# Three PSUM banks for scores, four for everything else, and one tile for a step's weights in a Perceiver cross-attention

## The chip, the core and the metric

The kernel runs on one core of one Trainium2 chip. The metric is the device time of one execution in microseconds (us), the median of several runs. A profile is one further execution, recorded instruction by instruction. Engines are named as the profile names them: PE (TensorE matmuls), PEld (TensorE weight loads), DVE (VectorE), ACT (ScalarE), POOL (GpSimd) and SP (SyncE, which issues most transfers).

## The reference, cut to what matters

The program is two layers of a Perceiver-like model over `x` of shape (4, 256, 256) with a context of shape (4, 4096, 192). Each layer is cross-attention to the context, a self-attention-like block, and a feed-forward block. The change touches only the first block, layer 0's cross-attention:

```python
x = x + _L0_xattn_ref(_layernorm(x), ctx_768, mask, Wq, Wk, Wv, Wo)
# 16 heads of 16 channels; for each of the 4 batches and each head:
#   scores  = (xn @ Wq) @ (ctx @ Wk).T / 4        256 tokens x 4096 context rows
#   weights = softmax(scores, masked rows left out)
#   out     = (weights @ (ctx @ Wv)) @ Wo
```

Everything is in float32.

## The kernel before, in words

**Units and steps.** `l0_xattn` cuts the work into 16 units: 4 batches times 4 groups of 4 heads. A unit's softmax needs the largest score of every token before it can exponentiate, so each unit's scores are computed twice. The first time (`ps_a`, tokens on the partitions, 512 context rows at a time) only the maximum of each row is kept (`mx`, L473). The second time (`ps_s`, context rows on the partitions, 256 tokens at a time) the negated maximum is already one of the rows of the query (`qb`), and ScalarE takes the exponential of what arrives (`e`, L469). These exponentials are the weights; they are multiplied with the values (`o_ps`, L406). One column of ones in the values gives the softmax's denominator.

**Half-steps.** One call of `step` is one sixteenth of a unit's exponentials and one sixteenth of another unit's maxima. The maxima run `LEAD` = 18 steps ahead of the exponentials, so the two belong to different units. `step` runs two halves, `hp` = 0 and `hp` = 1. A half has, on TensorE and in this order: the first score matmul of two heads (`weigh(0)`), one maxima matmul of each of the two other heads, the second score matmul of the first two heads (`weigh(1)`), and then `sums(hp)`, the four matmuls that multiply weights of the *previous* step with values. The four heads of a unit lie on the four groups of 32 rows of the systolic array, so the scores of two heads and the maxima of two others can stream through the array side by side. After the matmuls of a half ScalarE takes two exponentials and VectorE two maxima.

**PSUM.** Of the eight banks, one (`acc`) gathers `o_ps`, and seven form a ring (`ring`, tag `mm`) that all others share: two `ps_s` and two `ps_a` in each half, and between the steps the pair `ps_k0`/`ps_k1` or `ps_v0`/`ps_v1` of a projection of the context (28 key parts and 56 value parts within the steps), the transposed maxima `ps_m`, the queries `ps_q`, the tokens `ps_t`, the denominators `den` and the output projection `ps_wo`. A tile's first matmul has to wait until the last reader of the tile that held its bank is done.

**Weights.** Each head of a step has a tile of its own, `e0` to `e3`, with two buffers each. `ew` is the list of the four.

**Who sets the order.** The kernel is written with a tile framework. It decides the order of each engine's instructions from the program's order and its own estimate of when buffers come free, gives each tile a buffer, and adds the semaphore waits. An instruction that has to wait for two engines is preceded by a separate wait instruction (EVENT_SEMAPHORE in the trace). [...]

**The start.** In the first 18 steps (`t` < 0) there are no exponentials: each step has four `ps_a` matmuls alone, and from the tenth of them on one part of the first values (`first_values`) follows each.

Of the kernel before, what the change touches and what calls it, by code (L numbers as in the profile page):

```python
# [11 lines left out]
F32 = mybir.dt.float32  # L12
# [4 lines left out]
AF = mybir.ActivationFunctionType  # L17
ALU = mybir.AluOpType
AX = mybir.AxisListType
PSUM = bass.MemoryType.PSUM  # L20

P = 128
B, S, D = 4, 256, 256
# [224 lines left out]
def l0_xattn(c, w):  # L248
# [8 lines left out]
    nc, tc = c.nc, c.tc  # L257
    W = 17
    LEAD = 18
    with ExitStack() as es:  # L260
        one = es.enter_context(tc.tile_pool(name="x0_one", bufs=1))
        ring = es.enter_context(tc.tile_pool(name="x0_ring", bufs=7, space=PSUM))
        acc = es.enter_context(tc.tile_pool(name="x0_acc", bufs=1, space=PSUM))
        two = es.enter_context(tc.tile_pool(name="x0_two", bufs=2))

        def bank(name):
            return ring.tile([P, 512], F32, tag="mm", name=name)
# [128 lines left out]
        def sums(k):  # L396

            if not late:
                return
            u, n, ew = late.pop(0)  # L400
            b, g = divmod(u, 4)
            if n == 0:
                o_pss[u] = acc.tile([P, 512], F32, tag="o", name="o_ps")
            for h in range(4):
                c0 = (n * 8 + 4 * (g % 2) + h) * W
                nc.tensor.matmul(  # L406
                    o_pss[u][32 * h : 32 * h + 32, :S],
                    vs[g // 2][:, c0 : c0 + 32],
                    ew[h][:, n % 2, :],
                    start=(n == 0),  # L410
                    stop=(n == GT - 1),
                )
            if n == GT - 1:
                finish(u)
# [3 lines left out]
        def finish(u):  # L418
            b, g = divmod(u, 4)
            on = one.tile([P, S], F32, tag=f"on{g}", name=f"on{g}")  # L420
            attn_finish(c, two, ring, o_pss.pop(u)[:, :S], on)
            ons.append(on)
            if g == 3:
                add_projected(c, ring, b, ons, w.wo)
                ons.clear()

        def step(s, a):

            ew = {}
            for hp in range(2):  # L430
                work = []
                ts, ta = {}, {}
                for j in range(2):
                    if s:
                        ts[2 * hp + j] = bank("ps_s")
                    if a:
                        ta[2 - 2 * hp + j] = bank("ps_a")

                def weigh(k):
                    u, kp = s  # L440
                    for h, ps in ts.items():
                        hs = slice(32 * h, 32 * h + 32)
                        ks = slice((2 * kp + k) * P, (2 * kp + k + 1) * P)
                        nc.tensor.matmul(  # L444
                            ps[:, k * S : (k + 1) * S],
                            kts[u % 4 // 2][hs, u % 2, ks],
                            qbs[u][hs, :],
                            start=True,
                            stop=True,
                        )  # L450

                if s:
                    weigh(0)
                if a:
                    u, tt, ch = a
                    for h, ps in ta.items():
                        hs = slice(32 * h, 32 * h + 32)
                        nc.tensor.matmul(  # L458
                            ps,
                            qas[u][hs, tt * P : (tt + 1) * P],  # L460
                            kts[u % 4 // 2][hs, u % 2, ch * 512 : (ch + 1) * 512],
                            start=True,
                            stop=True,
                        )
                if s:
                    weigh(1)
                    for h, ps in ts.items():
                        e = two.tile([P, 2, S], F32, tag=f"e{h}", name=f"e{h}")
                        nc.scalar.activation(e, ps.rearrange("p (k n) -> p k n", k=2), AF.Exp)  # L469
                        ew[h] = e  # L470
                if a:
                    for h, ps in ta.items():
                        nc.vector.tensor_reduce(mxs[u][:, tt, h, ch : ch + 1], ps, AX.X, ALU.max)  # L473
                sums(hp)
            if s:
                late.extend((s[0], 2 * s[1] + k, ew) for k in range(2))

        n = 16 * 16
# [5 lines left out]
        for t in range(-LEAD, n):  # L484
            if t < 0:
                i = t + LEAD
                if i in (0, 2):
                    next(first_keys, None)
                if i == 3:
                    w.others()  # L490
                    for j in range(2):
                        nc.gpsimd.memset(kts[1][:, j, :], 1.0)
                if i > 8:
                    next(first_values, None)
            u, kp = divmod(t, 16)
            ua, ka = divmod(t + LEAD, 16)
            if ua < 16 and ka == 0 and ua > 0:
                queries(ua)
            if ua < 15 and ka == 8 and ua % 4 == 3:
                tokens(ua // 4 + 1)  # L500
            step((u, kp) if t >= 0 else None, (ua, ka % 2, ka // 2) if ua < 16 else None)
            if ua < 16 and ka == 15:
                with_largest(ua)
            if u in projections:
                steps, nb, ngp = projections[u]
                if kp == 0 and u % 2 == 0:
                    mask(nb, ngp)
                if kp % 2 == 0 if u % 2 else kp % 4 == 0:
                    next(steps, None)
        for _ in range(2):  # L510
            sums(0)
# [1376 lines left out]
def program(tc, a, out):  # L1888
# [3 lines left out]
    with ExitStack() as es:  # L1892
# [17 lines left out]
        with tc.tile_pool(name="w_a0", bufs=1) as pool_a0:  # L1910
            with tc.tile_pool(name="w_x0", bufs=1, side="right") as pool:
                w = l0_xattn_weights(c, pool)
                l0_xattn(c, w)
                w_a0 = l0_attn_weights(c, pool_a0)
            pool_f0 = es.enter_context(ExitStack())
            w_f0 = l0_ffn_weights(c, pool_f0.enter_context(tc.tile_pool(name="w_f0", bufs=1, side="right")))
            with tc.tile_pool(name="s4", bufs=1, side="right") as pool:
                l0_attn(c, w_a0, partial(s4d_kernel, c, pool))
# [148 lines left out]
```

## Time and profile before

| | |
|---|---|
| time, three runs | 2672.54 us median (2669.84 to 2682.69) |
| profiled execution: its own time | 2677.02 us |
| profiled execution: span from first to last instruction | 2674.9 us |
| the first 18 steps, maxima alone (about) | 25 to 102 us of the span |
| steps with scores and maxima | 102 to 1212 us |
| last steps, scores alone | 1212 to 1274 us |
| granted TensorE clock, 102 to 1274 us | 1.00 |
| 102 to 1274 us: busy PE, DVE, ACT | 1145.1, 663.0, 625.2 of 1171.9 us |
| exponentials (L469) | 1024, 594 ns each |
| maxima (L473) | 1024, 686 ns each |

The span is counted from the first instruction to the last; the time of a run has about 2 us more. A matmul in float32 is recorded as two passes, so counts of matmuls in the profile are twice those of the program. A row of the timeline merges neighbouring instructions of one kind: it gives the start of the first, the time from the first start to the last end, and the count. In brackets stands the idle time of that engine before the row and which engine's event ended it. The ends of matmuls are modelled.

### The profile page before, as it was taken

How to read it: one execution, taken by the hardware profiler on the slowest of the kernel's cores; microseconds unless marked ns; L12 is line 12 of the kernel's file. 1: busy time of each engine (PE TensorE's matmuls, PEld its weight loads, DVE VectorE, ACT ScalarE, POOL GpSimd, SP SyncE). 2: the span in 40 equal slices, each digit the busy share in tenths (PEclk: the TensorE clock that was granted, in tenths of full speed). 3: DMA queues.
4: the chain of work that ended last, by engine and by line, in shares of the span. 5: the costliest groups of instructions: out<-in, count | busy, mean ns of one | idle time of the engine just before them, and what ended most of it. 6: DMA issues, size and time to landing. Idle time of an engine off the chain costs nothing. (4 is left out here: it accounts for less than half of the span.)

```text
span 2674.9 us, 47755 instructions
## 1 busy us (share of the span) xinstructions
PE 2420.3 (90%) x19345; PEld 1419.5 (53%) x19345; DVE 1618.9 (61%) x3881; ACT 1095.0 (41%) x1913; POOL 179.1 (7%) x202
## 2 busy tenths in 40 slices
PE   8999999999999999999768989888999898984896
PEld 4445454545545454544435544466776777453554
DVE  6655655565565655561784440898798892735554
ACT  1355555555455555556111211555555562010221
POOL 3000000000000000000030000001010011412000
PEclk7899999999999999999888999799999999996876
DMA  7221213121221212100100012210303012100110
GB/s 197 76 53 58 61 50 80 38 73 45 62 56 55 63 37 73 45 2 1 43 1 1 5 47 67 79 60 20 99 22 97 6 50 96 55 0 16 33 24 8
DMA packets 63186, 130.78 MB, mean 49 GB/s; under 512 B 11584, under 2 KB 38912, under 8 KB 62512
## 3 DMA queue, kind: packets, MB, share of 16 engines
q1 hardware_dynamic: 61344, 123.73, 16.4%
q8 instruction: 154, 2.52, 0.4%
q10 hardware_dynamic: 1104, 2.88, 0.4%
q0 software_dynamic: 512, 1.05, 0.2%
q14 instruction: 72, 0.59, 0.1%
HBM read 97.12 MB, written 5.34 MB: 38 GB/s over the span
## 5 line engine op out<-in xcount | busy, mean ns | idle before, releaser
L473 DVE TENSOR_REDUCE mx<-ps_a 128x1 f32<-128x512 f32 x1024 | 658.3, 686 | 436.1 <-PE ps_a L458 436.1
L469 ACT ACTIVATE e<-ps_s 128x512 f32<-128x512 f32 x1024 | 555.8, 594 | 382.5 <-PE ps_a L458 356.5
L458 PE MATMUL ps_a<-kt,qa 32*128 32x512 f32 x2048 | 636.2, 653 | 1.9 <-DMA kt<-ks 0.8
L444 PE MATMUL ps_s<-qb,kt 32*128 32x256 f32 x4096 | 585.9, 401 | 0.0
L444 PEld LDWEIGHTS ps_s<-qb,kt 32*128 32x128 f32 x4096 | 348.7, 184 | 212.4 <-issue 94.2
L406 PE MATMUL o_ps<-e,v 128*32 128x256 f32 x4096 | 327.6, 391 | 0.0
L1152 PEld LDWEIGHTS ps_w<-diag,e 128*128 128x128 f32 x2048 | 238.8, 197 | 23.5 <-issue 21.5
L1152 PE MATMUL ps_w<-diag,e 128*128 128x128 f32 x2048 | 244.5, 281 | 0.4 <-POOL diag L1139 0.4
L458 PEld LDWEIGHTS ps_a<-kt,qa 32*128 32x128 f32 x2048 | 220.6, 186 | 20.9 <-DVE mx L473 7.8
L1109 DVE MAX8 cand<-sc 128x8 f32<-128x128 f32 x1024 | 212.2, 275 | 8.7 <-ACT sc L1097 8.7
L406 PEld LDWEIGHTS o_ps<-e,v 128*32 128x32 f32 x4096 | 81.0, 108 | 239.5 <-issue 229.5
L1133 DVE SCALAR_TENSOR_TENSOR e<-sc,top,e 128x1024 f32<-128x1024 f32 x128 | 159.1, 1279 | 28.5 <-ACT e L1124 28.5
L1124 ACT ACTIVATE e<-sc,neg 128x1024 f32<-128x1024 f32 x128 | 143.1, 1147 | 33.3 <-PE ps_w L1152 29.1
L1097 ACT COPY sc<-ps_s 128x1024 f32<-128x1024 f32 x128 | 126.3, 1007 | 41.9 <-PE ps_s L1088 39.6
L1166 PEld LDWEIGHTS ps_c<-cx,wT 128*128 128x128 f32 x512 | 86.1, 196 | 27.2 <-ACT wT L1160 11.3
L1166 PE MATMUL ps_c<-cx,wT 128*128 128x193 f32 x512 | 97.1, 341 | 1.9 <-ACT wT L1160 1.9
L335 ACT COPY v<-ps_v 128x256 f32<-128x256 f32 x128 | 41.4, 375 | 137.0 <-PE ps_v L325 137.0
L322 PE MATMUL ps_v<-x_wv,ctxT 128*128 128x128 f32 x512 | 92.8, 305 | 0.0
L322 PEld LDWEIGHTS ps_v<-x_wv,ctxT 128*128 128x128 f32 x512 | 69.4, 195 | 35.3 <-DVE mx L473 21.8
L1088 PE MATMUL ps_s<-kt,q 32*128 32x512 f32 x512 | 85.4, 647 | 0.0
L889 POOL MEMSET s_low<- 128x128 f32 x2 | 0.3, 206 | 1241.1 <-DVE x L188 1241.1
L301 ACT COPY ks<-ps_k 128x512 f32<-128x512 f32 x64 | 34.4, 589 | 111.4 <-PE ps_k L298 97.7
(403 smaller groups left out, 2735.6 us busy)
## 6 DMA issues: line engine op xcount, KB each, us to landing
ctxT<-in_ctxT SPq DMA_DIRECT2D x78, 768.0 KB
kt<-ks SPq DMA_DIRECT2D x352, 64.0 KB
cx<-in_ctx SPq DMA_DIRECT2D x16, 768.0 KB
x_w<-in_x_w SPq DMA_DIRECT2D x2, 1024.0 KB
qk<-rot SPq DMA_DIRECT2D x8, 256.0 KB
a_qk<-qk SPq DMA_DIRECT2D x16, 128.0 KB
ctxT<-in_ctxT ACTq DMA_DIRECT2D x2, 768.0 KB
x<-in_x SPq DMA_DIRECT2D x4, 256.0 KB
```

What stands on the lines that cost most here:

```text
L322: nc.tensor.matmul(ps[:, ks], ctxT[:, k0 : k0 + P], w.wv[:, 0, gs], start=True, stop=False)
L406: nc.tensor.matmul(o_pss[u][32 * h : 32 * h + 32, :S], vs[g // 2][:, c0 : c0 + 32], ew[h][:, n % 2, :], start=(n == 0), stop=(n == GT - 1),)
L444: nc.tensor.matmul(ps[:, k * S : (k + 1) * S], kts[u % 4 // 2][hs, u % 2, ks], qbs[u][hs, :], start=True, stop=True,)
L458: nc.tensor.matmul(ps, qas[u][hs, tt * P : (tt + 1) * P], kts[u % 4 // 2][hs, u % 2, ch * 512 : (ch + 1) * 512], start=True, stop=True,)
L469: nc.scalar.activation(e, ps.rearrange("p (k n) -> p k n", k=2), AF.Exp)
L473: nc.vector.tensor_reduce(mxs[u][:, tt, h, ch : ch + 1], ps, AX.X, ALU.max)
L1097: nc.scalar.copy(t, ps)
L1109: nc.vector.max(cands[u][:, n, :], sc[u][c4][:, i // 4, (i % 4) * P : (i % 4 + 1) * P])
L1124: nc.scalar.activation(t, src, AF.Exp, bias=neg)
L1133: nc.vector.scalar_tensor_tensor(t, src, top[:, 31:32], t, ALU.is_ge, ALU.mult)
L1152: nc.tensor.matmul(ps[:, i * P : (i + 1) * P], e[c4][:, half, i * P : (i + 1) * P], diag, start=(h == 0), stop=(h == 3),)
L1166: nc.tensor.matmul(ps_c[:, : DC + 1], wT[:, i * P : (i + 1) * P], cxs[b][t][:, j, :], start=(n == 0), stop=(n == 31))
```

## The change

It has two parts, both in `l0_xattn`.

1. The ring of seven banks becomes two pools. `three` has three banks and holds only the score tiles `ps_s`. `ring` keeps four banks and holds everything else: maxima, projections, transposed maxima, queries, tokens and denominators.
2. The four weight tiles `e0` to `e3` become one tile `e` of four heads per step, again with two buffers, so the memory is the same. The exponentials write, and the sums read, slices of it.

An unused list is removed too. The rest of the program is unchanged. Line numbers move by one at most: L406, L444 and L458 become L407, L445 and L459, the exponential stays L469, and the maximum L473 becomes L472.

```diff
-        ring = es.enter_context(tc.tile_pool(name="x0_ring", bufs=7, space=PSUM))
+        ring = es.enter_context(tc.tile_pool(name="x0_ring", bufs=4, space=PSUM))
+        three = es.enter_context(tc.tile_pool(name="x0_s", bufs=3, space=PSUM))
...
-                    ew[h][:, n % 2, :],
+                    ew[:, h, n % 2, :],
...
-            ew = {}
+            if s:
+                ew = two.tile([P, 4, 2, S], F32, tag="e", name="e")
             for hp in range(2):
-                work = []
                 ts, ta = {}, {}
                 for j in range(2):
                     if s:
-                        ts[2 * hp + j] = bank("ps_s")
+                        ts[2 * hp + j] = three.tile([P, 512], F32, tag="s", name="ps_s")
                     if a:
                         ta[2 - 2 * hp + j] = bank("ps_a")
...
                     for h, ps in ts.items():
-                        e = two.tile([P, 2, S], F32, tag=f"e{h}", name=f"e{h}")
-                        nc.scalar.activation(e, ps.rearrange("p (k n) -> p k n", k=2), AF.Exp)
-                        ew[h] = e
+                        nc.scalar.activation(ew[:, h, :, :], ps.rearrange("p (k n) -> p k n", k=2), AF.Exp)
```

## The prediction, made before the changed kernel had run

> **What bounds the kernel now.** I read the page first (who is busy), then the busy time by stretch, then the timeline of one plain stretch, then the built programs' waits.
>
> ```profile
> PE 2420.3 (90%) x19345; PEld 1419.5 (53%) x19345; DVE 1618.9 (61%) x3881; ACT 1095.0 (41%) x1913; POOL 179.1 (7%) x202
> L473 DVE TENSOR_REDUCE mx<-ps_a 128x1 f32<-128x512 f32 x1024 | 658.3, 686 | 436.1 <-PE ps_a L458 436.1
> L469 ACT ACTIVATE e<-ps_s 128x512 f32<-128x512 f32 x1024 | 555.8, 594 | 382.5 <-PE ps_a L458 356.5
> ...
> 102.15:1212.00 1109.85, 1084.87 (x10766) 558.48 (x10764) 659.48 (x1025) 585.36 (x1132) 0.00 (x0) 1.00 0.20 54
> ```
>
> VectorE and ScalarE both idle until TensorE delivers. In the 1110 us of steps with scores and maxima PE is busy 1085 at full granted clock, so TensorE sets the pace; but overlapped matmuls look busy while a later one waits, so I went to the timeline. These rows are two halves of a plain step:
>
> ```profile
> 599.93 0.48 PE L444 MATMUL ps_s<-qb,kt 32*128 32x256 f32 x2
> 599.94 0.70 PE L458 MATMUL ps_a<-kt,qa 32*128 32x512 f32 x2
> 600.47 0.59 PE L458 MATMUL ps_a<-kt,qa 32*128 32x512 f32 x2
> 600.68 0.38 PE L444 MATMUL ps_s<-qb,kt 32*128 32x256 f32 x2
> 601.10 1.29 DVE L473 TENSOR_REDUCE mx<-ps_a 128x1 f32<-128x512 f32 x2 [0.61 <-PE ps_a L458]
> 601.24 1.09 ACT L469 ACTIVATE e<-ps_s 128x512 f32<-128x512 f32 x2 [0.59 <-PE ps_a L458]
> 601.57 0.48 PE L444 MATMUL ps_s<-qb,kt 32*128 32x256 f32 x2
> 601.58 0.95 PE L458 MATMUL ps_a<-kt,qa 32*128 32x512 f32 x2
> 602.32 0.38 PE L444 MATMUL ps_s<-qb,kt 32*128 32x256 f32 x2
> 602.38 0.59 PE L458 MATMUL ps_a<-kt,qa 32*128 32x512 f32 x1
> 603.11 1.09 ACT L469 ACTIVATE e<-ps_s 128x512 f32<-128x512 f32 x2 [0.78 <-PE ps_a L458]
> 603.47 0.48 PE L444 MATMUL ps_s<-qb,kt 32*128 32x256 f32 x2
> ```
>
> Half A (hp 0) goes from 599.93 to 601.57: 1.64 us, nothing waits. Half B (hp 1) takes to 603.47: 1.90. Its two first `ps_a` passes are spread over 0.95 instead of 0.70 us: the second maxima matmul waits 0.26. The built program says for what: its bank is released by the *previous* half's first maximum (601.10 + 0.69 = 601.79, and the matmul starts 0.05 later). B's maximum starts later in the half, so the next A does not wait. A plain step is 1.64 + 1.90 = 3.54 us, of which 0.26 is this wait.
>
> **What the change does to the waits.** In the built changed program each bank's release can be followed. The maxima now reuse banks of two halves before, so the 0.26 us wait is gone. But each half takes two of three score banks, so in *every* half the second score matmul reuses the bank of the previous half's *first* score, and waits for its exponential. That is later than the first maximum: B's matmuls start at 601.57, the previous exponential has only begun at 601.24.
>
> What is queued behind: the second score matmul is second of a half's ten; both maxima, both `weigh(1)` and the sums follow it. TensorE lets nothing past:
>
> ```profile
> 846.01 0.29 PEld L458 LDWEIGHTS ps_a<-kt,qa 32*128 32x128 f32 x3 [0.35 <-DVE qa L377]
> 846.12 0.19 PEld L444 LDWEIGHTS ps_s<-qb,kt 32*128 32x128 f32 x2
> ```
>
> Here `ps_a` waited until 846.01 for new queries, and the weights of the next score matmul, on other rows of the array, came only after it (846.12 is 0.76 after the half's start, where 0.32 is normal). So the delay d of the second score matmul moves the whole half: its length is 1.63 + d.
>
> The value of d. The exponential starts 601.24, 1.31 after half A's start; one lasts 0.60 (merged two: 1.09); the release reaches TensorE 0.05 later, which these rows show (0.38 + 0.05 between copy and matmul):
>
> ```profile
> 859.35 0.38 ACT L169 COPY o_sb<-o_ps 128x256 f32<-128x256 f32 x1
> 859.78 0.70 PE L171 MATMUL den<-o_sb,sel 128*128 128x256 f32 x2 [0.97 <-ACT o_sb L169]
> ```
>
> 601.24 + 0.60 + 0.05 = 601.89, against 601.57: d = 0.32 in half B, had A been followed as in the changed kernel. If A was delayed itself, its exponential (which waits for the last maximum too, see the rivals) and its end move alike, so d stays. For half A the weights' tile matters. Before, nearly every exponential has a separate wait instruction (1016 of 1024), since it also waits for the earlier writer of its `e` buffer; after, in the built program, only the first of each step has (254). Half B's exponentials lose it. With it, ACT starts 0.14 to 0.18 us after the last maximum matmul's end (602.97 to 603.11; 601.06 to 601.24). Without it the nearest row is the copy of the values, 0.03 after its matmul (61.80 to 61.83, below). I take 0.07, since A's three near-simultaneous completions cost 0.03 more than B's: d = 0.32 - 0.10 = 0.22 in half A. Bounds: 0.15 (no latency at all) to 0.25.
>
> **The sum.** Laid out half by half over the timeline, this stretch has 237 halves A and 237 B. 135 A follow a B directly, 102 follow projections and the like (the exponential is then long done, d = 0); 102 B stand before such work.
>
> - 135 A and the 135 B before plain halves: now 478.2 us together (135 x 3.54). After: A 1.63 + 0.22 = 1.85, B 1.63 + 0.32 = 1.95, so 135 x 3.81 = 514. **+36**
> - 102 B before other work: 1.95 for 1.90. **+6**
> - Last 18 steps, scores alone, 1.63 a half, no waits now. Without maxima an exponential does not move with d, so what one half waits the next is spared: about 0.3 per step. **+5**
> - The start. With projections of values between maxima, now:
>
> ```profile
> 61.31 0.49 PE L325 MATMUL ps_v<-x_wv,ctxT 64*128 64x128 f32 x4
> 61.73 1.14 PE L458 MATMUL ps_a<-kt,qa 32*128 32x512 f32 x8
> 61.83 0.65 ACT L335 COPY v<-ps_v 128x256 f32<-128x256 f32 x2 [4.13 <-PE ps_v L325]
> 62.80 0.71 PE L322 MATMUL ps_v<-x_wv,ctxT 128*128 128x128 f32 x4
> 62.89 2.48 DVE L473 TENSOR_REDUCE mx<-ps_a 128x1 f32<-128x512 f32 x4 [1.35 <-PE ps_a L458]
> ```
>
> One step is 3.20 us (1.07 maxima, 2.13 values). Four `ps_a` and two `ps_v` fitted into seven banks; into four they do not. The values' second bank now waits for the step's second maximum. From its release: 1.80 of values left, 1.13 maxima, 0.04 wake, 0.61 + 0.68 for two maxima, 0.05: 4.31 instead of 3.20. Seven such steps: +8. Before them VectorE is the bound (0.6 us a maximum) and TensorE runs seven banks ahead; now four, so values start three maxima later: +2. **+10**
>
> Costed at nothing: the shared `e` tile. A buffer is reused every second step, and its last readers are the sums of the step just before, which TensorE has issued ahead of this step's first matmul; ScalarE starts 1.3 us after that. The sums read it by head (only the fourth waits, for an exponential done 0.5 us before). Were this a whole-tile wait, it would be the same exponential. Fourteen times the next half's scores move ahead of `den`; `den` waits about 1 us for ScalarE and the maxima still set the half's length: 0; if not covered, 0.5 x 14 = 7. SP's and POOL's order is unchanged, ScalarE has room (1.09 us of a half's 1.64).
>
> 36 + 6 + 5 + 10 = 57. The profiled execution would go from 2677.0 (span 2674.9) to 2734; its 4.5 us over the median of the runs stays, so **2672.5 + 57 = 2730**.
>
> **A rule weighed.** In the rows above the weights behind a waiting matmul wait with it. The Trainium skill ("TensorE: Matmul & The Clock Gate", Step-by-step: what each phase is for) says that TensorE pulls weight loads ahead of matmuls in flight when the row groups do not conflict. If that held during the wait, each delayed half would get back one load, 0.10 (the first two `ps_s` passes are 0.32 apart, later ones 0.22): 372 x 0.10 = 37, so +20 instead of +57. The trace's 846.12 speaks against it for an instruction waiting on a semaphore, so I keep 57 and leave 2693 in the range.
>
> **Rivals.**
> 1. *The change does what it seems to: the wait goes and none comes (not slower).* Mechanism: the exponential is released by its own score matmul, and the bank when its data are read (0.49, the spacing of two), not at its end (0.60). Own matmul ends 1.13 after the half's start whatever d is; 1.13 + 0.12 + 0.49 + 0.05 - 1.63 = 0.16 for a step's two d together. It decides where the two sum to under 0.27, the wait removed. Then 135 x -0.10 and 102 x -0.11, with +13 for start and end: -11, 2661; with the end at 0.60 about 2686. Against: in half B own scores end at 602.70, the maxima at 602.97, and ACT starts 603.11. It followed the maxima, which come earlier in TensorE's count.
> 2. *Weight loads run ahead:* 2693, above.
> 3. *Worse:* d 0.35 and 0.25 (more simultaneous completions), +53; end and start +7 and +15, the `den` reordering +5: +80, 2752.
> 4. *The change does not do what it says:* the built program shows three and four banks, and the wait instructions gone; excluded.
>
> **How the numbers follow.** About 0.5%, 13 us, is what a measurement of this kernel tells from no change. Forecast and its spread (2708 to 2752) 0.83; rival 2 and mixtures above 2686, 0.09; rival 1 0.08, of it 0.02 faster by over 13 us, 0.06 within. The bounds of d alone (0.15/0.26 to 0.25/0.35) make +27 to +75. Range 2697 to 2752.
>
> **What would show it.** Right: in plain stretches halves of about 1.85 and 1.95 us; the second `ps_s` weight load 0.2 to 0.3 after the first in every half; both `ps_a` of a half starting together; exponentials of half B starting under 0.1 after the last maximum; 102 becoming about 112, and the block's end 1274 about 1331; all later stages as long as before. Wrong: A and B at 1.64, or exponentials starting before the maxima end.

## Result: 3.3% slower, and the profile after

The changed kernel takes 2763.66 us (median of 6 runs, 2754.7 to 2772.19); the kernel before, on the same chip, 2671.95 us. The ratio is 1.0333, with a 95% interval of 1.0315 to 1.0352. The prediction was 2730 (2697 to 2752): the direction and the new wait were right, the size was not, and the time lies above the range. The profiled execution took 2763.01 us, its span is 2760.9 us against 2674.9. Some executions take a slower course at a lower mean clock (none of the kernel before's or the changed kernel's, but 1 of 6 of "busier start" and of "score matmul moved" below, 5 of 20 of "moved, values in score banks" and 4 of 14 of the last kernel), and every ratio leaves them out.

The page's busy rows after, and the groups that answer to those shown of before:

```profile
PE 2521.0 (91%) x19345; PEld 1536.0 (56%) x19345; DVE 1619.9 (59%) x3881; ACT 1094.6 (40%) x1913; POOL 184.6 (7%) x202
L472 DVE TENSOR_REDUCE mx<-ps_a 128x1 f32<-128x512 f32 x1024 | 659.4, 685 | 528.1 <-PE ps_a L459 527.8
L469 ACT ACTIVATE e<-ps_s 128x512 f32<-128x512 f32 x1024 | 555.7, 594 | 446.8 <-PE ps_a L459 417.2
```

No instruction of VectorE or ScalarE became longer: a maximum still takes 685 ns, an exponential 594. VectorE's idle time ahead of the maxima grew by 92 us (436.1 to 528.1), ScalarE's by 64: both wait longer for TensorE. TensorE's busy time grew by 101 us with the same 19345 records; since overlapping matmuls are merged, most of that is waiting that looks like work, and in the start, below, the passes themselves are longer.

The timeline of a plain stretch shows the wait:

```profile
619.90 1.09 ACT L469 ACTIVATE e<-ps_s 128x512 f32<-128x512 f32 x2 [0.87 <-PE ps_a L459]
620.23 0.81 PE L445 MATMUL ps_s<-qb,kt 32*128 32x256 f32 x3
620.56 0.19 PEld L459 LDWEIGHTS ps_a<-kt,qa 32*128 32x128 f32 x2
620.56 0.70 PE L459 MATMUL ps_a<-kt,qa 32*128 32x512 f32 x2
...
621.09 0.59 PE L459 MATMUL ps_a<-kt,qa 32*128 32x512 f32 x2
...
621.80 1.08 ACT L469 ACTIVATE e<-ps_s 128x512 f32<-128x512 f32 x2 [0.81 <-PE ps_a L459]
...
622.19 0.74 PE L445 MATMUL ps_s<-qb,kt 32*128 32x256 f32 x2
622.46 0.70 PE L459 MATMUL ps_a<-kt,qa 32*128 32x512 f32 x2
...
624.09 0.48 PE L445 MATMUL ps_s<-qb,kt 32*128 32x256 f32 x1
```

A half starts at 620.23 and its maxima only at 620.56; before, both started together. In between stands the second score matmul, which waits for the first exponential of the half before: 619.90 + 0.60 + 0.05 = 620.55. In the next half it is 0.27 (622.19 to 622.46; 621.80 + 0.60 + 0.05 = 622.45). The halves last 1.96 and 1.90 us, where they lasted 1.90 (B) and 1.64 (A). Both maxima now start together, so the wait of before is gone, as predicted.

The start went worse than predicted. This is one step with projections of values, and the first maxima of the next:

```profile
69.13 2.87 PE L459 MATMUL ps_a<-kt,qa 32*128 32x512 f32 x8
71.23 2.48 DVE L472 TENSOR_REDUCE mx<-ps_a 128x1 f32<-128x512 f32 x4 [4.30 <-PE ps_a L459]
71.98 1.10 PEld L323 LDWEIGHTS ps_v<-x_wv,ctxT 128*128 128x128 f32 x4 [1.56 <-DVE mx L472]
73.30 0.80 PE L326 MATMUL ps_v<-x_wv,ctxT 64*128 64x128 f32 x4
75.92 2.87 PE L459 MATMUL ps_a<-kt,qa 32*128 32x512 f32 x8
```

The weights of the first value bank wait 1.56 us for the first maximum, and those of the second bank wait again: instruction by instruction they start at 72.58, 0.05 after the second maximum ends (72.52). That is the predicted wait. But the step takes 6.79 us, not 4.31, and each pass is longer than before: four `ps_v` passes of L326 take 0.80 us, where they took 0.49. The busy time by stretch says why. Its columns are busy time with counts of PE, PEld, DVE, ACT and POOL, then the granted clock, the DMA share and GB/s; first two stretches of before, then two of after:

```profile
43.00:57.00 14.00, 14.00 (x50) 9.37 (x46) 12.21 (x27) 0.00 (x0) 0.00 (x0) 0.50 0.84 213
65.00:78.00 13.00, 13.00 (x100) 8.04 (x104) 10.15 (x17) 2.77 (x9) 0.00 (x0) 1.00 0.35 126
```

```profile
62.00:103.00 41.00, 41.00 (x148) 25.37 (x146) 14.89 (x24) 3.88 (x12) 0.00 (x0) 0.50 0.18 58
114.00:128.00 14.00, 12.98 (x44) 7.07 (x44) 8.02 (x13) 2.17 (x4) 0.00 (x0) 0.50 0.12 47
```

In both kernels the clock is at half in the last stretch of maxima ahead of the values. Before, it reached full some 7 us after the values had begun (53.19); after, it stayed at half until 128. In 62 to 103 PE looks busy all the time: this column tells neither a half clock nor a half empty array from work. Part of the array does wait: in the step above the third and fourth maxima matmul start 0.53 and 0.80 us after the first (69.65 and 69.93), each 0.05 after ScalarE's copy out of a value bank has ended.

Cut at the first plain half and at the last half of the last steps, the 86.0 us of the spans lie here (start, block, rest):

| part | before | after | difference | predicted |
|---|---|---|---|---|
| start, to the first plain half | 102.2 | 129.9 | +27.7 | +10 |
| plain halves A (136) | 1.64 | 1.90 (100), 2.09 (36) | +40.8 | +28 |
| plain halves B (135) | 1.89 | 1.96 | +9.4 | +8 |
| halves B before other work | | | +11 | +6 |
| other halves of the block | | | about 0 | 0 |
| last steps, scores alone | | | +3.3 | +5 |
| all later stages | 1402.8 | 1396.8 | -6.0 | 0 |

The code of the later stages is untouched; in the twelve profiles of this study they last from 1389 to 1406 us, so their 6 us mean nothing.

### The profile page after: what moved, and what is told of

It reads as the page before. It is cut to its first block, busy times and chain, and to the rows that moved or that the text cites. A ratio compares the mean times of both kernels' runs of the same rounds, so it can differ in the third digit from the quotient of the medians.

```text
span 2760.9 us, 46976 instructions
## 1 busy us (share of the span) xinstructions
PE 2521.0 (91%) x19345; PEld 1536.0 (56%) x19345; DVE 1619.9 (59%) x3881; ACT 1094.6 (40%) x1913; POOL 184.6 (7%) x202
## 5 line engine op out<-in xcount | busy, mean ns | idle before, releaser
L472 DVE TENSOR_REDUCE mx<-ps_a 128x1 f32<-128x512 f32 x1024 | 659.4, 685 | 528.1 <-PE ps_a L459 527.8
L469 ACT ACTIVATE e<-ps_s 128x512 f32<-128x512 f32 x1024 | 555.7, 594 | 446.8 <-PE ps_a L459 417.2
L445 PE MATMUL ps_s<-qb,kt 32*128 32x256 f32 x4096 | 707.3, 403 | 0.5 <-ACT e L469 0.5
L459 PE MATMUL ps_a<-kt,qa 32*128 32x512 f32 x2048 | 600.3, 669 | 1.7 <-DVE mx L472 1.6
L445 PEld LDWEIGHTS ps_s<-qb,kt 32*128 32x128 f32 x4096 | 465.7, 184 | 225.7 <-PE ps_a L459 91.8
L407 PE MATMUL o_ps<-e,v 128*32 128x256 f32 x4096 | 327.3, 391 | 0.0
L459 PEld LDWEIGHTS ps_a<-kt,qa 32*128 32x128 f32 x2048 | 176.4, 190 | 31.1 <-DVE mx L472 16.0
L407 PEld LDWEIGHTS o_ps<-e,v 128*32 128x32 f32 x4096 | 80.9, 108 | 195.4 <-issue 194.6
L1165 PE MATMUL ps_c<-cx,wT 128*128 128x193 f32 x512 | 100.1, 348 | 2.9 <-ACT wT L1159 2.9
L323 PE MATMUL ps_v<-x_wv,ctxT 128*128 128x128 f32 x512 | 99.4, 321 | 0.0
L1138 POOL TENSOR_SCALAR diag<-ident,r 128x128 f32<-128x128 f32 x32 | 55.3, 1728 | 430.9 <-DVE r L1136 340.7
```

Source lines behind the costliest of these rows:

```text
L323: nc.tensor.matmul(ps[:, ks], ctxT[:, k0 : k0 + P], w.wv[:, 0, gs], start=True, stop=False)
L407: nc.tensor.matmul(o_pss[u][32 * h : 32 * h + 32, :S], vs[g // 2][:, c0 : c0 + 32], ew[:, h, n % 2, :], start=(n == 0), stop=(n == GT - 1),)
L445: nc.tensor.matmul(ps[:, k * S : (k + 1) * S], kts[u % 4 // 2][hs, u % 2, ks], qbs[u][hs, :], start=True, stop=True,)
L459: nc.tensor.matmul(ps, qas[u][hs, tt * P : (tt + 1) * P], kts[u % 4 // 2][hs, u % 2, ch * 512 : (ch + 1) * 512], start=True, stop=True,)
L469: nc.scalar.activation(ew[:, h, :, :], ps.rearrange("p (k n) -> p k n", k=2), AF.Exp)
L1165: nc.tensor.matmul(ps_c[:, : DC + 1], wT[:, i * P : (i + 1) * P], cxs[b][t][:, j, :], start=(n == 0), stop=(n == 31))
```

## Experiments

All ratios are to the kernel before; those of the experiments are from 5 rounds beside it. "Start" and "block" are cut as above, from one profile each; "seven steps" is the sum of the seven start steps with values, the last of which holds other work too.

| kernel | ratio (95%) | start | block | seven steps | plain halves A, B |
|---|---|---|---|---|---|
| before | 1 | 102.2 | 1169.9 | 31.5 | 1.64, 1.90 |
| after | 1.0333 (1.0315 to 1.0352) | 129.9 | 1234.2 | 51.8 | 1.90, 1.96 |
| banks only | 1.0385 (1.0357 to 1.0414) | 138.3 | 1243.7 | 51.8 | 1.96, 1.96 |
| tile only | 0.9991 (0.9972 to 1.0010) | 100.1 | 1169.1 | 31.3 | 1.64, 1.90 |
| values in score banks | 1.0264 (1.0239 to 1.0289) | 109.5 | 1233.9 | 29.8 | 1.90, 1.96 |
| busier start | 1.0314 (1.0285 to 1.0343) | 120.8 | 1234.2 | 41.9 | 1.90, 1.96 |
| score matmul moved | 1.0216 (1.0171 to 1.0260) | 128.5 | 1181.6 | 51.7 | 1.64, 1.96 |
| moved, values in score banks | 1.0044 (1.0028 to 1.0061) | 113.7 | 1181.4 | 29.8 | 1.64, 1.96 |
| four banks for scores | 1.0281 (1.0256 to 1.0306) | 150.8 | 1201.5 | 62.7 | 1.90, 1.64 |
| start on seven banks | 1.0228 (1.0215 to 1.0242) | 104.7 | 1234.3 | 29.9 | 1.90, 1.96 |
| start on seven, moved | 1.0019 (1.0007 to 1.0030) | 101.8 | 1181.6 | 28.1 | 1.64, 1.96 |
| the same with the copy | 1.0001 (0.9991 to 1.0011) | 102.1 | 1168.5 | 30.5 | 1.65, 1.89 |

**Which part of the change.** Banks only keeps one weight tile per head; tile only keeps the ring of seven.

```diff
# banks only, against after
-            if s:
-                ew = two.tile([P, 4, 2, S], F32, tag="e", name="e")
+            ew = {}
...
+                        e = two.tile([P, 2, S], F32, tag=f"e{h}", name=f"e{h}")
...
# tile only, against after
-        ring = es.enter_context(tc.tile_pool(name="x0_ring", bufs=4, space=PSUM))
-        three = es.enter_context(tc.tile_pool(name="x0_s", bufs=3, space=PSUM))
+        ring = es.enter_context(tc.tile_pool(name="x0_ring", bufs=7, space=PSUM))
...
-                        ts[2 * hp + j] = three.tile([P, 512], F32, tag="s", name="ps_s")
+                        ts[2 * hp + j] = bank("ps_s")
```

> Only the banks are divided (three for scores, four for the rest); a step's weights stay in four tiles, one per head. Theory (the divided banks make every half's second score matmul wait for the exponential of the half before; the single tile only takes a separate wait instruction of about 0.1 us off some of ScalarE's exponentials): the halves with maxima for one head pair lose a little more than in the changed kernel, because the exponential starts 0.14 to 0.18 us behind the last maxima matmul instead of 0.11 to 0.12; about 7 us more than the changed kernel, 2771 us, ratio 1.036 to the kernel before. Rival (the single tile costs as much as the banks, by holding all four weights of a step in one dependency): about half of the 91 us goes, 2715 to 2730 us, ratio 1.016 to 1.022.

> Only the tile is changed (a step's four weights in one tile); all seven banks stay in one ring. Theory (the banks carry the whole loss): the time of the kernel before, 2668 to 2678 us, ratio 0.998 to 1.002, and maximum releases the halves as before. Rival (the single tile costs as much as the banks): 2700 to 2725 us, ratio 1.010 to 1.020.

Tile only runs like the kernel before. Banks only is slower than after: its halves A grew to 1.96, and its block is 9.5 us longer than that of after, where 7 was expected (the ratio differs by 0.005, some 14 us, of which the start of the profile has 8). So the banks carry the whole loss, and the single tile gives a little back, as it takes the separate wait instruction off half B's exponentials. The rival in both expectations is out.

**The start: banks or clock?**

```diff
# values in score banks
-                    pss = [bank("ps_v0"), bank("ps_v1")]
+                    if first:
+                        pss = [three.tile([P, 512], F32, tag="s", name=f"ps_v{j}") for j in range(2)]
+                    else:
+                        pss = [bank("ps_v0"), bank("ps_v1")]
# busier start
                 if i > 8:
+                    fill = three.tile([P, 512], F32, tag="s", name="fill")
+                    nc.tensor.matmul(fill, c.ident, w.wq[:, 0, :], start=True, stop=True)
                     next(first_values, None)
```

(`first` is true for the first values alone, those of the start.)

> The changed kernel, but the values' projections of the start take the three score banks, which stand empty there, instead of the four that the maxima use. Theory (the start lost its 27.7 us because a projection of values and four maxima share four banks, so the projection's weight load waits for a maximum of the same step): the first mixed half begins at about 102 us again instead of 130, the granted clock between 62 and 102 us is near 1.0, and the whole is 28 us faster than the changed kernel, about 2736 us, ratio 1.023. Rival (the start is held by what feeds it, keys and context from DMA, and not by banks): within 5 us of the changed kernel, ratio 1.032 to 1.034.

> The changed kernel with one more 512-column matmul per half of a start step without scores, ahead of its maxima, into a score bank that nothing reads: work added, none removed, and the waits for banks stay. Theory of the clock (the waits leave TensorE so little work there that its granted clock stays at 0.50, and the half clock is most of the loss of the start): granted clock near 1.0 between 62 and 103 us, a start step with values 4.3 to 4.5 us instead of 6.8, and the whole 15 to 20 us faster than the changed kernel, about 2745 us, ratio 1.027. Theory of waits alone (the clock is a mere companion): the start is as long as in the changed kernel or up to 10 us longer, 2763 to 2774 us, ratio 1.033 to 1.037.

With the values in the score banks the seven steps take 29.8 us again. The timeline of TensorE in this kernel has the step without a wait at the half clock, and then the change to the full one:

```profile
65.52 2.09 PE L462 MATMUL ps_a<-kt,qa 32*128 32x512 f32 x8
67.54 1.22 PE L326 MATMUL ps_v<-x_wv,ctxT 128*128 128x128 f32 x4
...
71.30 2.09 PE L462 MATMUL ps_a<-kt,qa 32*128 32x512 f32 x8
73.32 0.71 PE L326 MATMUL ps_v<-x_wv,ctxT 128*128 128x128 f32 x4
```

From 65.52 to 71.30 the step is 5.78 us at half clock; later, at full clock, it is 3.20 (79.13 to 82.33), as before. So of the 3.59 us that a step of after lost, 2.58 are the half clock and only 1.01 (6.79 - 5.78) the wait; the prediction had the wait at 1.11. Here the clock also came later than expected (0.50 from 62 to 73, where near 1.0 was expected), and so did the first plain half (109.5 for 102).

The busier start tests whether waits and half clock are cause and effect. The kernel that ran has one extra matmul per start step from the tenth on, not one per half as its expectation says. The scheduler put the first three of them early, at 22 to 34 us, so the first steps with values are unchanged; from 83.84 on there is one in each step:

```profile
81.04 2.87 PE L459 MATMUL ps_a<-kt,qa 32*128 32x512 f32 x8
83.84 1.82 PE L494 MATMUL fill<-x_wq,ident 128*128 128x512 f32 x2
85.50 0.61 PE L323 MATMUL ps_v<-x_wv,ctxT 128*128 128x128 f32 x4
86.03 0.49 PE L326 MATMUL ps_v<-x_wv,ctxT 64*128 64x128 f32 x4
86.45 0.71 PE L323 MATMUL ps_v<-x_wv,ctxT 128*128 128x128 f32 x4
87.52 1.92 PE L459 MATMUL ps_a<-kt,qa 32*128 32x512 f32 x8
```

With the first of them the clock goes to full (granted 0.50 from 74.26 to 81.04, 1.00 from 85.50 to 102.02; 0.49 for the L326 passes), and the steps go from 6.79 to 4.83 us although they have more to do. Only the last four of the seven steps ran whole at the full clock. The whole gained 8 us on after (by the ratios 5) instead of 15 to 20, and its interval overlaps that of after, so the steps of the profile decide here and not the total. Added work made TensorE faster: the waits-only theory is out for these steps.

Values in the score banks gained 20 us where 28 were expected. What was left stood ahead of the values:

```diff
# start on seven banks
         def bank(name):
+            if begun[0] >= 0:
+                begun[0] += 1
+                if begun[0] % 7 > 3:
+                    return three.tile([P, 512], F32, tag="s", name=name)
             return ring.tile([P, 512], F32, tag="mm", name=name)
```

(`begun[0]` becomes -1 at the first step with scores.)

> The changed kernel, but the whole start (until the first scores) deals its tiles round all seven banks, as before the change; nothing is left out. Theory (the start's loss has two parts: 20 us in the seven steps with values, which the score banks for values take away alone, and 7 to 10 us in the maxima before them, where VectorE waits for TensorE because only four banks are in flight): the first plain half begins at 100 to 104 us, the maxima before the values end at about 55 to 57 us instead of 62, the whole 24 to 28 us under the changed kernel, 2736 to 2740 us, ratio 1.023 to 1.025. Rival (the early part is the arrival of the keys by DMA, which differs from run to run): no gain over values in the score banks alone, 2742 to 2746 us, ratio 1.026.

It came out at 1.0228, by the ratios 28 us under after and 10 us under values in the score banks, and the first plain half is at 104.7. The maxima before the values ended at 61 us, not at 55 to 57. Over all profiles the time from the first maximum to the first start step with values is 33 to 39 us in the five kernels with seven banks there, 40 to 44 in the six with four, 48 in the one with three. It has two parts. Up to the end of the second keys' projection it is 7 to 16 us with seven banks and 14 to 19 with fewer; kernels with the same number of banks differ here by as much as 9 us, so how much of this the banks cost stays open. From there on it is 22 to 26 us with seven, 25 to 27 with four and 30 with three, a loss of 2 to 3 us, about what the prediction had put. The rival's "no gain" is not what came, but of the gain only these 2 to 3 us can be put down to the banks.

**The block: what passes the delay on?**

```diff
# score matmul moved
-                    weigh(0)
+                    weigh(0, list(ts.items())[:1])
...
-                    weigh(1)
+                    weigh(0, list(ts.items())[1:])
+                    weigh(1, ts.items())
```

> The changed kernel with one matmul moved: the second head's first score matmul of a half is issued behind the two maxima matmuls instead of ahead of them. Nothing is left out, banks and tile are the changed kernel's. Theory (the second score matmul waits for a bank; the maxima queued behind it are late by the same time, and since exponentials count TensorE's work in program order, an exponential waits for late maxima and passes the delay on to the next half): a step's two delays sum to about 0.24 us, as in the last steps without maxima, instead of 0.59; a plain step of 3.50 to 3.55 us instead of 3.86; the whole 45 to 50 us faster than the changed kernel, about 2716 us, ratio 1.015 to 1.018, the start as long as in the changed kernel. Rival (the delay is the exponential's own length and does not depend on what is queued behind): a plain step stays 3.8 to 3.9 us, ratio 1.031 to 1.034.

> The moved score matmul and the values' projections of the start in the score banks together; nothing is left out. Theory (start and order of the score matmuls are all of the loss, and they add up): the seven start steps with values 30 us together as in the kernel before instead of 52, a plain step 3.50 to 3.55 us, the whole within 10 us of the kernel before, 2665 to 2685 us, ratio 0.997 to 1.005. Rival (part of the loss lies in neither): 2690 us or more, ratio above 1.007.

> The start on seven banks and the second head's first score matmul behind the maxima, without the copy. Theory: plain halves of 1.64 and 1.96 us, the start at 100 to 104 us; 10 us less than with values in the score banks and the same order, 2676 to 2684 us, ratio 1.001 to 1.004. Rival (early part is DMA): 2686 to 2694 us, ratio 1.004 to 1.006.

With one matmul behind the maxima instead of ahead of them, half A is back at 1.64 us and the block 52.6 us shorter. Here the maxima start with the half, and only the score matmul waits (kernel with the start on seven banks):

```profile
621.49 1.09 ACT L476 ACTIVATE e<-ps_s 128x512 f32<-128x512 f32 x2 [3.60 <-PE ps_a L465]
621.81 0.48 PE L451 MATMUL ps_s<-qb,kt 32*128 32x256 f32 x1
621.82 0.70 PE L465 MATMUL ps_a<-kt,qa 32*128 32x512 f32 x2
622.13 0.59 PE L451 MATMUL ps_s<-qb,kt 32*128 32x256 f32 x3
...
623.08 1.09 ACT L476 ACTIVATE e<-ps_s 128x512 f32<-128x512 f32 x2 [0.50 <-PE ps_a L465]
...
623.76 0.48 PE L451 MATMUL ps_s<-qb,kt 32*128 32x256 f32 x1
```

The maxima of the delayed half (B) end in time, the exponential starts at 623.08, 1.27 after the half's start at 621.81, and is done just before the next half needs the bank (623.08 + 0.60 + 0.05 = 623.73). So the delay is not the exponential's length alone: it was carried from half to half by the maxima behind the waiting matmul, which the exponentials count (in the trace maxima and score matmuls count up the same semaphore, and the exponentials wait for it). That rival is out. The 36 halves A of 2.09 us are gone too. In after, TensorE has two separate wait instructions there, for the landing of key tiles, behind the blocked matmul. In this half A the first maxima pass starts 0.37 after the half (133.81), where 0.27 is normal, the next 0.13 later, and the half lasts until 135.53:

```profile
133.44 0.74 PE L445 MATMUL ps_s<-qb,kt 32*128 32x256 f32 x3
133.81 0.79 PE L459 MATMUL ps_a<-kt,qa 32*128 32x512 f32 x2
```

The theory missed one thing: a plain step became 3.60 us, not 3.50 to 3.55. Half B still waits 0.32: the half A before it is only 1.64 long, and its first exponential is done 1.98 us after A's start (1.33 + 0.60 + 0.05). About 0.05 of that comes from the separate wait instruction ahead of A's exponentials, which is tested next. The first of the three kernels came out at 1.0216, above its band; the five times behind it lie between 2709 and 2748 us, and its profile, of the fastest of them, is 53.6 us shorter than that of after, more than the 45 to 50 expected. So the longer step does not explain the ratio, and why the times spread so far is open. The other two are inside their bands (1.0044 and 1.0019), and show that start and order add up.

**The separate wait instruction.** A copy of eight constants into spare columns of the weights' tile takes that wait, early in the step:

```diff
-                ew = two.tile([P, 4, 2, S], F32, tag="e", name="e")
+                ep = two.tile([P, 8 * S + 8], F32, tag="e", name="e")
+                nc.scalar.copy(ep[:, 8 * S :], c.cols[:, 0:8])
+                ew = ep[:, : 8 * S].rearrange("p (h k n) -> p h k n", h=4, k=2)
```

> Three things together on top of the changed kernel: the whole start (until the first scores) deals its tiles round all seven banks as before the change, the second head's first score matmul stands behind the maxima, and a step's weights' tile has eight more columns, into which ScalarE copies eight constants that nothing reads, so that the wait for the tile's earlier writer falls on this copy and no longer on the first exponential. Theory (the separate wait instruction makes the first half's exponentials 0.05 to 0.08 us later, and all of it reaches the next half): the second half of a plain step 1.88 to 1.91 us instead of 1.96, about 12 us less than the same kernel without the copy; 2660 to 2674 us, ratio 0.995 to 1.000. Rival (the exponential's start is set by the landing of the four matmuls it counts, not by the wait instruction): 1.95 us as without the copy, 2675 to 2690 us.

```profile
619.96 0.48 PE L453 MATMUL ps_s<-qb,kt 32*128 32x256 f32 x1
621.23 1.08 ACT L478 ACTIVATE e<-ps_s 128x512 f32<-128x512 f32 x2 [0.56 <-PE ps_a L467]
621.85 0.48 PE L453 MATMUL ps_s<-qb,kt 32*128 32x256 f32 x1
622.20 0.20 ACT L438 COPY e<-cols 128x8 f32<-128x8 f32 x1
623.50 0.48 PE L453 MATMUL ps_s<-qb,kt 32*128 32x256 f32 x1
```

The copy sits in idle time of ScalarE (622.20), the delayed half lasts 1.89 us (619.96 to 621.85), and the block is 13.1 us shorter than without the copy, where 12 were expected; the rival's 1.95 is out. In the times the gain is smaller: 1.0019 to 1.0001, about 5 us; the later stages, the same code, are 10 us longer in this profile. By the ratio the divided banks and the single tile now cost nothing that can be measured: 1.0001 (0.9991 to 1.0011), just outside the band. They gain nothing either: no version of this study beats the kernel before.

**The division turned round.**

```diff
-        ring = es.enter_context(tc.tile_pool(name="x0_ring", bufs=4, space=PSUM))
-        three = es.enter_context(tc.tile_pool(name="x0_s", bufs=3, space=PSUM))
+        ring = es.enter_context(tc.tile_pool(name="x0_ring", bufs=3, space=PSUM))
+        three = es.enter_context(tc.tile_pool(name="x0_s", bufs=4, space=PSUM))
```

(on top of values in score banks)

> The division turned round: four banks for scores, three for maxima and projections, the values of the start in the score banks; the order of the changed kernel, nothing left out. Theory (eight banks are wanted for two halves and seven are there, so one matmul per half must wait for the half before; what it costs is set by which reader it waits for): no score matmul waits any more, the second maxima matmul waits for the half before's first maximum as in the kernel before, halves of 1.64 and 1.90 us; other work between the halves finds one bank less and adds 0 to 0.3 us in each of about 100 places; 2670 to 2700 us, ratio 0.999 to 1.010. Rival (any fixed division costs like the changed one, because a class cannot borrow from the other): plain halves of 1.9 us or more both, 2740 us or more, ratio above 1.024.

The plain halves are 1.64 and 1.90 us, those of the kernel before, as the theory said, but now A is the one that waits: other work ahead of an A delays it, and after that every second half waits. The total is nearer to the rival, 1.0281, for two reasons that the theory had too small. Halves after other work grew by 0.48 us each (1.74 to 2.22 on average, 88 of them): behind values the second maxima matmul starts 0.52 after its half instead of 0.02, when the copy has ended (0.47) that frees a projection's bank. And in the start the four maxima of a step no longer fit their three banks:

```profile
80.91 2.08 PE L462 MATMUL ps_a<-kt,qa 32*128 32x512 f32 x6
83.02 1.89 DVE L475 TENSOR_REDUCE mx<-ps_a 128x1 f32<-128x512 f32 x3 [5.07 <-PE ps_a L462]
83.76 2.07 PE L462 MATMUL ps_a<-kt,qa 32*128 32x512 f32 x2 [0.77 <-DVE mx L475]
85.76 1.22 PE L326 MATMUL ps_v<-x_wv,ctxT 128*128 128x128 f32 x4
89.52 2.08 PE L462 MATMUL ps_a<-kt,qa 32*128 32x512 f32 x6
```

TensorE rests 0.77 us in every step, the clock stays at half past 130 us, and the step is 8.61 us.

## Why the prediction fell short

- **The new wait: right.** In every plain half the second score matmul waits for the exponential of the half before, and everything behind it moves. Half B was predicted at 1.95 and measured 1.96.
- **Half A: mis-sized.** The step "d = 0.22" failed. It took 0.07 us from the last maxima matmul of a half B to its exponential; the trace has 0.12 (621.68 to 621.80), so d is 0.27, the upper end of the bounds plus 0.02. In 36 of the 136 halves two wait instructions for key tiles, covered before, stand behind the blocked matmul and add 0.19. Together +13 us. (The sum has a slip, 3.81 for 1.85 + 1.95 = 3.80, worth 1 us; and by its own terms the bounds of d give about +31 to +66, not +27 to +75.)
- **B before other work: mis-sized.** The step "1.95 for 1.90" overlooked that the 15 halves before the transposed maxima end in a wait for the last maximum, which moves by the whole d: from half to `ps_m`, 2.77 became 3.09 us. Here +5 us.
- **The start: the step "4.31 instead of 3.20" failed.** The chain of waits was right, the clock of its terms was not: it took the start's rows at the full clock that they happened to have. At half clock 1.80 of values left become 3.34 (72.58 to 75.92) and 1.13 of maxima 2.07; with 0.04, 1.29 for two maxima and 0.05 the same chain gives the measured 6.79. The waits were worth 1.01 us a step against 1.11, the half clock 2.58. The clock column stood in the view by stretch that the prediction began with (0.65 in 23 to 57 us, 0.81 in 57 to 102); it was read for the block and not for the start. The seven steps lost 20 us where 8 were predicted: five of them 3.59 each, the first and the last, which held other work or the half clock before too, 2.3 together. The maxima ahead of them lost 7 (39.9 for 33.2) where 2 were predicted, and about half of these 7 lie in the keys' part that one profile can't size. Together with smaller pieces +18.
- **Weight loads run ahead (rival 2): out.** The weights behind a waiting matmul waited with it in every delayed half (above, both start at 620.56).
- **"Costed at nothing": right.** The tile alone is 0.9991 (0.9972 to 1.0010), and the 14 moved `den` cost about 1 us.

A rule on the clock bears on the step that failed. The Trainium skill ("TensorE: Matmul & The Clock Gate", Part 1) says that the gate passes either half or all pulses, and goes to full after about 3.4 us of sustained work. The trace agrees on the two values. On the time it does not: the kernel before reached 1.00 only some 7 us after its values began without a wait, and a step of after, with 5.78 us of work (the step without a wait) in each 6.79, stayed at 0.50 from 62 to 103 us. What counts as sustained in such a rhythm no run here shows, so the rule alone would not have decided between the two clocks. What each makes of the time: at full clock the sum is 2730; with a step of 6.79 in place of 4.31 for seven steps it has +17 more, 2747 with everything else as it was.

## What to carry to other kernels

Count the banks that two neighbouring halves want: here eight, with seven there, so at least one matmul in each pair of halves waits for the half before, in one ring as in both divisions tried. What can be chosen is which reader it waits for and what stands behind it in the engine's order; put the matmul that will wait behind those that start with it, and a wait stays in its half instead of going round. Before a pool is cut, look for the stages that borrow from it (here the start, where one class stood empty), and check at which clock a stage ran that is about to get a wait.

## What was not expected of the hardware

- With waits worth about 1 us in each step of 6.79 us TensorE stayed at 0.50 from 62 to 103 us, though no stretch of that time looks idle; one extra matmul in each step brought 1.00 within 2 us and a step of 4.83 us. With the values in the score banks, without the waits, it went to full as well (0.99 from 73 to 89 us).
- A separate wait instruction ahead of an exponential made it about 0.05 us later than a wait carried by the exponential itself (half A without and with the copy: 1.33 against 1.27 after the half's start). Two of them ahead of TensorE's maxima cost 0.1 us each as soon as a wait stood ahead of them, and nothing before.
- Where score and maxima matmuls are issued in between each other and count up one semaphore, an exponential waits for maxima that it does not read. Moving one matmul by two places took 52.6 us off the block.
